# Relative positions in attention: 32 windows of the table against one row of queries each, or the whole tables against all queries and a diagonal read from DRAM

## The chip, the core and the metric

The kernel runs on one core of a Trainium2 chip. The metric is the device time of one execution in microseconds (us), taken over several runs. The engines are TensorE (PE, with its weight loads PEld), VectorE (DVE), ScalarE (ACT), GpSimd (POOL) and SyncE (SP, which issues most of the DMAs).

## The reference

The input `x` is 8 images of 32 x 32 positions with 384 channels. Layer 0 is a group norm, then self-attention over all 1024 positions of an image with 6 heads of 64, and a residual. The score has two relative terms, one for rows and one for columns:

```python
attn  = einsum('bqd,bkd->bqk', q * SCALE, k)
Rh    = rel_pos_h[i - j + 31]          # (32, 32, 64), a row per (query row i, key row j)
Rw    = rel_pos_w[i - j + 31]
rel_h = einsum('bhwc,hkc->bhwk', q, Rh)   # query (h, w) with key row k
rel_w = einsum('bhwc,wkc->bhwk', q, Rw)   # query (h, w) with key column k
attn[h, w, kh, kw] += rel_h[h, w, kh] + rel_w[h, w, kw]
out   = softmax(attn) @ v @ proj_w + proj_b
```

Layer 1 is a layer norm with causal attention over the 1024 tokens (one head of 384), and for the first five images an FFN of 384 x 1536 with binarized weights and a rescaling by the largest absolute value. The position tables have 63 rows of 64 each. A term depends on the query and on the difference of the two coordinates alone, so each query needs its product with 32 of the 63 rows.

## The kernel before, in words

The kernel works through the images one after the other in `run`. For each: `layer0` (projections, relative positions, attention), `attention1`, for images 0 to 4 `ffn`, and four DMAs on SP that store the result (L857). `between` normalises the next image in the middle of `attention1`. The order of instructions on each engine is fixed when the program is built, and it need not be that of the code: in the trace, some query projections of an image run while the FFN of the image before is still going on. Each engine then takes its own queue in order.

In `layer0`, `queries_keys(m)` projects 128 columns of queries (m = 0 to 2) or keys (m = 3 to 5), two heads at a time (a pair `p`; `par` is the head within the pair). L429 (ScalarE) rounds the product to float32r, and L430 (VectorE) stores what the rounding left. So `q[par]` has a rounded part in one half of its 128 partitions and the rest in the other half, and so have the keys. L442 and L443 (POOL) copy the keys with the halves exchanged (`ks`).

`positions(g)` takes four rows (d = 0) or columns (d = 1) of queries. For each of the four, for both heads and both tables, one plain fp32 matmul (L454) multiplies a window of 32 rows of the table with 96 queries (32 positions of the three pairs) and writes 32 partitions of PSUM. That is 16 matmuls per group and 128 per image. Then L464 (ScalarE) rounds the result to float32r and L465 (VectorE) stores the rest, both into `r[par]`, four times each per group, 32 times each per image. `values(j)` projects 128 positions of `v`, copied out of PSUM by L470, on ScalarE and VectorE in turn.

`attend0_fast` takes the pairs one after the other. For each 128 keys (a chunk `c`) and each head, L508 makes scores of 128 x 1024 in PSUM with three float32r matmuls per half: keys with queries, exchanged keys with queries, and `unit` with `r`. `unit` (made on POOL by `make_unit`) is a 0/1 matrix that gives each key its row's and its column's term. L512 takes the exponential on ScalarE, L521 sums on VectorE, and L526 multiplies with `v`. Two score tiles (`s_tile`, two banks of PSUM each) and four tiles of one bank (`o_tile`) exist; the position products use an `o_tile`. `page` is a pool of eleven SBUF tiles of 128 x 1024, used by the exponentials, the sums and, in the FFN, by the rounded activations. SP also loads the residual (L105), and the next image (L294). In the FFN's end, POOL clamps the output (L834), and VectorE adds it (L835), after which the stores L857 go out.

Of the kernel before, what the change touches and what calls it, by code (L numbers as in the profile page):

```python
# [17 lines left out]
P = 128  # L18
B, H, W, C = 8, 32, 32, 384
T = H * W  # L20
NJ = T // P
NC = C // P
NH, HD = 6, 64
NPAIR = NH // 2
# [50 lines left out]
def conv_attn_hybrid(  # L75
# [19 lines left out]
    nc = tc.nc  # L95
    assert GSB == 1
    const = ctx.enter_context(tc.tile_pool(name="const", bufs=1))
# [10 lines left out]
    def tile_of(name, shape):  # L108
        return const.tile(shape, F32, name=name)
# [1 line left out]
    wqkv_sb, wproj_sb, wv_sb = (tile_of(n, [P, NC, w]) for n, w in (("wqkv_sb", 3 * C), ("wproj_sb", C), ("wv_sb", C)))  # L111
    bqk, bv, b1_sb = (tile_of(n, [P, w]) for n, w in (("bqk", 6), ("bv", NC), ("b1_sb", NM)))
    pb, b2_sb = tile_of("pb", [P, C]), tile_of("b2_sb", [P, C])
    rel = tile_of("rel", [P, 2, 2 * H - 1])
    qscale = HD**-0.5

    def load_weights():

        nc.scalar.dma_start(out=bqk, in_=qkv_b[0 : 2 * C].rearrange("(m p) -> p m", p=P))
        for half in range(2):  # L120
            nc.scalar.dma_start(out=rel[half * HD : (half + 1) * HD, 0, :], in_=rel_hT)
            nc.scalar.dma_start(out=rel[half * HD : (half + 1) * HD, 1, :], in_=rel_wT)
        nc.scalar.dma_start(out=bv, in_=qkv_b[2 * C : 3 * C].rearrange("(m p) -> p m", p=P))
        nc.scalar.dma_start(out=b1_sb, in_=b1.rearrange("(m p) -> p m", p=P))
        src = qkv_w.rearrange("(k p) o -> p k o", p=P)
        for i in range(3):
            nc.sync.dma_start(out=wqkv_sb[:, :, ts(i, C)], in_=src[:, :, ts(i, C)])
        nc.sync.dma_start(out=wproj_sb, in_=proj_w.rearrange("(k p) o -> p k o", p=P))
        nc.sync.dma_start(out=pb, in_=proj_b.partition_broadcast(P))
        nc.sync.dma_start(out=wv_sb, in_=wv.rearrange("(k p) o -> p k o", p=P))  # L130
        nc.sync.dma_start(out=b2_sb, in_=b2.partition_broadcast(P))

        nc.scalar.mul(wqkv_sb[:, :, 0:C], wqkv_sb[:, :, 0:C], qscale)
        nc.scalar.mul(bqk[:, 0:NPAIR], bqk[:, 0:NPAIR], qscale)
        nc.scalar.mul(rel, rel, 1.0 / qscale)


    ident = const.tile([P, P], F32, name="ident")
# [8 lines left out]
    fold = const.tile([P, 2, 32], F32, name="fold")  # L147
    for i in range(2):
        nc.vector.tensor_reduce(fold[:, i, :], ident.rearrange("p (k i) -> p i k", k=4), AX.X, ALU.add)
    ones = const.tile([P, P], F32, name="ones")  # L150
    nc.gpsimd.memset(ones, 1.0)

    to_group = const.tile([P, NC, GROUPS_GN], F32, name="to_group")
# [21 lines left out]
    def make_unit():  # L175

        for i in range(4):
            r = slice(32 * i, 32 * (i + 1))
            nc.gpsimd.tensor_copy(
                unit[r].rearrange("i (h w) -> i h w", h=H), ident[r, r].unsqueeze(2 - i % 2).to_broadcast([32, H, W])  # L180
            )


# [3 lines left out]

    def judge(pools):

        bad = const.tile([P, 2, N_SEEN], F32, name="bad")  # L190
# [89 lines left out]
    def stages(pools):  # L280
# [140 lines left out]
        def layer0(b, xT):  # L421

            q, k, ks, r = ([pools.image(f"{n}_{b}_{par}", F32R) for par in range(2)] for n in ("q", "k", "ks", "r"))

            def hi_lo(dst, hi, lo, ps, bias):
                nc.scalar.activation(dst[hi], ps[hi], AF.Identity, bias=bias[hi])  # L429
                nc.vector.scalar_tensor_tensor(dst[lo], ps[hi], bias[hi], dst[hi].bitcast(F32), ALU.add, ALU.subtract)  # L430

            rows = (slice(0, HD), slice(HD, P))

            def queries_keys(m):
                p = m % NPAIR
                ps = project_T(wqkv_sb, ts(m, P), xT, f"qk_{b}_{m}")
                for par in range(2):
                    hi, lo = rows[par], rows[1 - par]
                    dst = (q if m < NPAIR else k)[par][:, p, :]
                    hi_lo(dst, hi, lo, ps, bqk[:, m : m + 1])  # L440
                    if m >= NPAIR:
                        nc.gpsimd.tensor_copy(ks[par][hi, p, :], dst[lo].bitcast(F32))  # L442
                        nc.gpsimd.tensor_copy(ks[par][lo, p, :], dst[hi].bitcast(F32))  # L443

            def positions(g):

                ps = pools.o_tile(f"rel_{b}_{g}")[:, :384].rearrange("p (i n) -> p i n", i=4)
                for i in range(4):
                    at = 4 * g + i
                    win = slice(H - 1 - at, 2 * H - 1 - at)  # L450
                    for par in range(2):
                        qv = q[par].bitcast(F32).rearrange("d p (h w) -> d p h w", h=H)
                        for d in range(2):
                            nc.tensor.matmul(  # L454
                                ps[ts(2 * par + d, 32), i, :], rel[:, d, win], qv[:, :, :, at] if d else qv[:, :, at, :],
                                start=True, stop=True,
                            )
                for d in range(2):
                    for par in range(2):
                        hi, lo = 2 * par + d, 2 * (1 - par) + d  # L460
                        dst = r[par].rearrange("k p (h w) -> k p h w", h=H)
                        dst = dst[:, :, :, ts(g, 4)] if d else dst[:, :, ts(g, 4), :]
                        src = ps[ts(hi, 32)].rearrange("k i (p t) -> k p t i" if d else "k i (p t) -> k p i t", p=NPAIR)
                        nc.scalar.copy(dst[ts(hi, 32)], src)  # L464
                        nc.vector.tensor_tensor(dst[ts(lo, 32)], src, dst[ts(hi, 32)].bitcast(F32), ALU.subtract)  # L465

            v = pools.flat(f"v0_{b}")[:, : NJ * C].rearrange("p (j c) -> p j c", j=NJ)

            def values(j):
                (nc.vector.tensor_copy if j % 2 else nc.scalar.copy)(  # L470
                    v[:, j, :], project(wqkv_sb, slice(2 * C, 3 * C), xT, j, f"v0_{b}_{j}")
                )

            for m in range(NPAIR):
                queries_keys(m)

            queries_keys(NPAIR)
            for g in range(NJ):
                positions(g)
                if g in (1, 3):  # L480
                    queries_keys(NPAIR + 1 + g // 2)
                values(g)
            if pools.fast and b == 0:
                join_biases(pools)
# [12 lines left out]
            return (attend0_fast if pools.fast else attend0_general)(residual, b, sides, v)  # L497

        def attend0_fast(residual, b, sides, v):
# [62 lines left out]
            def finish(p, sums, avs):  # L562

                tr = pools.page(f"tr0_{b}_{p}")
                for half in range(2):
                    den = pools.o_tile(f"den0_{b}_{p}_{half}")
                    for par in range(2):
                        nc.tensor.matmul(  # L568
                            den[ts(par, HD), :], ones[:, :HD], sums[par][:, ts(half, 512)], start=True, stop=True
                        )  # L570
# [266 lines left out]
        def run(pools):  # L837
            gn = load_T(0)
            if pools.fast:
                load_weights()  # L840
            gn = group_norm_T(0, gn)
            if pools.fast:
                make_unit()
# [62 lines left out]
```

## Time and profile before

| | |
|---|---|
| time, median of three runs | 2678.16 us (2672.93 to 2678.53) |
| the profiled execution | 2677.02 us, of which the span of the trace 2675.2 us |
| TensorE busy | 2574.3 us, 96% of the span |
| VectorE, ScalarE, POOL busy | 1496.3, 1056.5, 215.6 us |
| granted TensorE clock | 0.99 of full speed |
| DMA | 82.0 MB, 31 GB/s over the span |

A group row names a line, an engine, an operation, the tile written and the tiles read with partitions x elements, the count, then the total busy time in us and the mean in ns of one instruction, and after the second bar the time that the engine sat idle just before it and for what. A wait row names who waited for whom, the total in us, the number of times and the longest. Tiles of the main path have the prefix f_. Two records of one matmul line can belong to one call: the count in a row is of records.

### The profile page before, as it was taken

Reading aid. Unit: us, or ns where it says so; the run is one execution under the profiler, and the core shown is the slowest. Engines: PE = TensorE matmul, PEld = TensorE weight load, DVE = VectorE, ACT = ScalarE, POOL = GpSimd, SP = SyncE. Lnnn points to the kernel's source line nnn. Section 1 sums busy time; section 2 is a strip of 40 time slices with the busy share of each in tenths; the row PEclk is TensorE's granted clock in tenths of the full one; section 3 lists DMA queues with packets and bytes.
Section 4 is the critical chain, followed back from the end, with each engine's and each line's share of the span. In section 5 each row is a group of like instructions: output and inputs, shape, how many; then the busy total and the mean of one; then the engine's idle time right before and its main releaser. Section 6 shows DMA issues by size and latency. Waiting matters only on the chain.

```text
span 2675.2 us, 28350 instructions
## 1 busy us (share of the span) xinstructions
PE 2574.3 (96%) x11394; PEld 1546.7 (58%) x11394; DVE 1496.3 (56%) x2368; ACT 1056.5 (39%) x1470; POOL 215.6 (8%) x202
## 2 busy tenths in 40 slices
PE   8989999999999999999999999999999999999998
PEld 4554585555765556755558555576555555555554
DVE  4885456663565644666545666346664356425652
ACT  3431274431555414654127443155541254115411
POOL 2010004000030000120000400003000020002000
PEclk9999999999999999999999999999999999999999
DMA  2501101010010101010110101001000100010000
GB/s 93 201 35 59 36 1 48 1 60 33 4 48 1 48 12 36 12 36 1 59 36 1 48 1 59 3 33 48 1 24 0 48 1 0 24 48 1 1 1 25
DMA packets 34572, 82.00 MB, mean 31 GB/s; under 512 B 5120, under 2 KB 27520, under 8 KB 32896
## 3 DMA queue, kind: packets, MB, share of 16 engines
q1 hardware_dynamic: 28496, 56.43, 5.9%
q0 software_dynamic: 2880, 23.59, 2.6%
q8 instruction: 92, 1.51, 0.2%
q10 hardware_dynamic: 3056, 0.08, 0.1%
q14 instruction: 48, 0.39, 0.0%
HBM read 62.79 MB, written 17.30 MB: 30 GB/s over the span
## 4 chain that ended last, share of the span: by engine, by line
PE 88%; DVE 6%; ACT 2%; issue 1%; POOL 1%; DMA 1%; ACTq 0%; SPq 0%; DVEq 0%
PE f_s L508 19%; PE f_av L526 12%; PE f_v L385 8%; PE f_qk L375 8%; PE f_s L680 7%; PE f_av L694 7%; PE f_y L784 6%; PE f_y L821 6%; PE f_q L659 5%; PE f_pj L385 4%; PE f_rel L454 3%; POOL f_y L834 1%; PE f_pt L287 1%; DVE f_r L465 1%; PE f_den L568 1%
## 5 line engine op out<-in xcount | busy, mean ns | idle before, releaser
L512 ACT ACTIVATE f_pr<-f_s 128x1024 f32<-128x1024 f32 x384 | 393.6, 1026 | 446.0 <-PE f_s L508 429.9
L521 DVE TENSOR_TENSOR f_sum<-f_sum,f_pr 128x1024 f32<-128x1024 f32 x288 | 355.4, 1247 | 228.6 <-ACT f_pr L512 226.7
L526 PE MATMUL f_av<-f_pr,f_v 128*64 128x512 f32 x1536 | 351.8, 598 | 0.0
L508 PE MATMUL f_s<-f_q,f_k 128*128 128x512 f32 x768 | 258.0, 415 | 13.2 <-ACT f_pr L512 13.1
L375 PE MATMUL f_qk<-f_gnT,wqkv_sb 128*128 128x512 f32 x576 | 265.4, 607 | 1.2 <-DVE f_gnT L336 1.2
L508 PE MATMUL f_s<-f_r,unit 128*128 128x512 f32 x768 | 242.8, 397 | 2.5 <-DVE f_r L465 2.5
L508 PE MATMUL f_s<-f_q,f_ks 128*128 128x512 f32 x768 | 242.4, 397 | 0.0
L526 PEld LDWEIGHTS f_av<-f_pr,f_v 128*64 128x64 f32 x1536 | 101.9, 136 | 200.0 <-issue 192.2
L680 PE MATMUL f_s<-f_q,f_lnT 128*128 128x512 f32 (+3 forms) x576 | 200.1, 491 | 0.0
L694 PE MATMUL f_av<-f_v,f_pr 128*128 128x385 f32 x576 | 194.5, 486 | 0.0
L508 PEld LDWEIGHTS f_s<-f_q,f_k 128*128 128x128 f32 x768 | 125.4, 189 | 118.8 <-issue 48.7
L375 PEld LDWEIGHTS f_qk<-f_gnT,wqkv_sb 128*128 128x128 f32 x576 | 108.3, 194 | 123.6 <-issue 121.3
L465 DVE TENSOR_TENSOR f_r<-f_rel,f_r 32x384 fp32r<-32x384 f32 x256 | 139.7, 553 | 52.7 <-ACT f_r L464 46.7
L508 PEld LDWEIGHTS f_s<-f_r,unit 128*128 128x128 f32 x768 | 144.0, 189 | 40.4 <-DVE f_r L465 6.8
L508 PEld LDWEIGHTS f_s<-f_q,f_ks 128*128 128x128 f32 x768 | 145.2, 189 | 35.0
L694 PEld LDWEIGHTS f_av<-f_v,f_pr 128*128 128x128 f32 x576 | 108.6, 190 | 78.6 <-issue 11.5
L680 PEld LDWEIGHTS f_s<-f_q,f_lnT 128*128 128x128 f32 x576 | 100.7, 190 | 71.5 <-issue 47.4
L464 ACT CAST f_r<-f_rel 32x384 fp32r<-32x384 f32 x256 | 118.8, 469 | 50.8 <-PE f_rel L454 26.3
L385 PE MATMUL f_v<-wqkv_sb,f_gnT 128*128 128x384 f32 x384 | 137.9, 495 | 0.0
L385 PE MATMUL f_pj<-wproj_sb,f_oT 128*128 128x384 f32 x384 | 128.1, 490 | 9.6 <-DVE f_oT L574 9.6
L788 ACT ACTIVATE f_h<-f_y,b_sb 128x256 f32<-128x256 f32 x240 | 101.7, 472 | 69.0 <-PE f_y L784 38.0
L659 PE MATMUL f_q<-f_lnT,wqk 128*128 128x512 f32 x288 | 127.9, 598 | 0.0
(156 smaller groups left out, 3371.2 us busy)
## 6 DMA issues: line engine op xcount, KB each, us to landing
f_gnT<-in_xT SPq DMA_DIRECT2D x24, 512.0 KB, 4.6
f_x<-in_x SPq DMA_DIRECT2D x32, 384.0 KB, 4.5
out_y<-f_x SPq DMA_DIRECT2D x32, 384.0 KB, 2.5
f_w1a<-w1s POOLq DMA_DIRECT2D x5, 1536.0 KB, 7.2
f_w2a<-w2s POOLq DMA_DIRECT2D x5, 1536.0 KB, 6.8
f_wrest<-w1s POOLq DMA_DIRECT2D x5, 768.0 KB, 4.6
f_wrest<-w2s POOLq DMA_DIRECT2D x5, 768.0 KB, 8.4
wqkv_sb<-in_qkv_w SPq DMA_DIRECT2D x3, 576.0 KB, 5.8
```

Of the source, the lines that this page charges most:

```text
L375: nc.tensor.matmul(ps[:, half, :], w[:, k, cols], xT[:, k, ts(half, 512)], start=(k == 0), stop=(k == NC - 1),)
L385: nc.tensor.matmul(ps[:, :C], xT[:, k, ts(j, P)], w[:, k, cols], start=(k == 0), stop=(k == NC - 1))
L465: nc.vector.tensor_tensor(dst[ts(lo, 32)], src, dst[ts(hi, 32)].bitcast(F32), ALU.subtract)
L508: nc.tensor.matmul(sc[:, half, :], keys[:, ts(c, P)], queries[:, ts(half, 512)], start=(i == 0), stop=(i == 2))
L512: nc.scalar.activation(pr, sc.rearrange("p a n -> p (a n)"), AF.Exp)
L521: nc.vector.tensor_tensor(sums[par], prev, prs[par], ALU.add)
L526: nc.tensor.matmul(avs[half][ts(par, HD), :], v[:, c, ts(h, HD)], prs[par][:, ts(half, 512)], start=(c == 0), stop=(c == NJ - 1),)
L659: nc.tensor.matmul(ps, wqk[:, k, ts(m, P)], xT[:, half, k, :], start=(k == 0), stop=(k == NC - 1))
L680: nc.tensor.matmul(sc[:, half, lo:], xT[:, c // 4, k, ts(c % 4, P)], q[:, half, k, lo:], start=(k == 0), stop=(k == NC - 1),)
L694: nc.tensor.matmul(av[:, : C + 1], prs[c][:, ts(j - c, P)], v[:, c, :], start=(c == 0), stop=(c == j))
L784: nc.tensor.matmul(ps, w1k[i // 2][:, ts(m, P)], xs[i % 2][:, half, i // 2, :], start=(i == 0), stop=(i == 2 * NC - 1))
L821: nc.tensor.matmul(ps[:, :C], hs[i][:, m, :], w2m[half * 6 + m], start=(half == m == i == 0), stop=(half == i == 1 and m == 5),)
```

## The change

The position products are no longer made window by window. `rel_split` holds both tables, 63 rows and one of zeros each, side by side as 128 columns, once rounded to float32r and once what the rounding left. `positions(p)` now works on a pair: for each head and each half of the positions, two float32r matmuls (one with each part of `rel_split`, summed in PSUM) multiply all 128 table rows with 512 queries. ScalarE copies the 64 rows of the first table to a page, and VectorE the 64 rows of the second, with the positions transposed so that columns come first. The page is stored to DRAM (`far`) by one DMA of 512 KB on SP. Then, for each head and table, one DMA on SP reads from `far` the diagonal of 32 x 32 pieces of 32 numbers that the 32 windows stand for, into a quarter of another page, `near`. A new function, `split`, rounds this to float32r on ScalarE and stores the rest on VectorE into `r`, once per pair, head and table, 1024 numbers per partition each. The diagonal gives the keys' coordinate in the opposite order, so `unit` is built reversed, and the tables are no longer reversed on the host.

In the order of the code, `positions(p)` stands after `queries_keys(p + 1)`, all key projections come before all of `values`, and the splits stand before `values(0)`, after `values(3)` and after `values(7)`. `ones` is cut to 64 columns, `bad` becomes a page, and `rel` a page of the start.

```diff
-    rel = tile_of("rel", [P, 2, 2 * H - 1])
+    rel_split = const.tile([P, 2, 2, 2 * H], F32R, name="rel_split")
...
+        rel = pools.page("rel")[:, : 4 * H].rearrange("p (d i) -> p d i", d=2)
+        nc.vector.memset(rel, 0.0)
...
         nc.scalar.mul(rel, rel, 1.0 / qscale)
+        nc.scalar.copy(rel_split[:, 0], rel)
+        nc.vector.tensor_tensor(rel_split[:, 1], rel, rel_split[:, 0].bitcast(F32), ALU.subtract)
...
-                unit[r].rearrange("i (h w) -> i h w", h=H), ident[r, r].unsqueeze(2 - i % 2).to_broadcast([32, H, W])
+                unit[r].rearrange("i (h w) -> i h w", h=H),
+                ident[r, r][:, ::-1].unsqueeze(2 - i % 2).to_broadcast([32, H, W]),
...
-            def positions(g):
-                ps = pools.o_tile(f"rel_{b}_{g}")[:, :384].rearrange("p (i n) -> p i n", i=4)
-                for i in range(4):
-                    at = 4 * g + i
-                    win = slice(H - 1 - at, 2 * H - 1 - at)
-                    for par in range(2):
-                        qv = q[par].bitcast(F32).rearrange("d p (h w) -> d p h w", h=H)
-                        for d in range(2):
+            def positions(p):
+                fars = []
+                for par in range(2):
+                    page = pools.page(f"far_{b}_{p}_{par}")
+                    by_col = page.rearrange("i (w h) -> i w h", h=H)
+                    for half in range(2):
+                        ps = pools.o_tile(f"rel_{b}_{p}_{par}_{half}")
+                        for i in range(2):
                             nc.tensor.matmul(
-                                ps[ts(2 * par + d, 32), i, :], rel[:, d, win], qv[:, :, :, at] if d else qv[:, :, at, :],
-                                start=True, stop=True,
+                                ps, rel_split[:, i].rearrange("d a n -> d (a n)"), q[par][:, p, ts(half, 512)],
+                                start=(i == 0), stop=(i == 1),
                             )
+                        nc.scalar.copy(page[:HD, ts(half, 512)], ps[:HD])
+                        nc.vector.tensor_copy(
+                            by_col[HD:, :, ts(half, H // 2)], ps[HD:].rearrange("i (h w) -> i w h", w=W)
+                        )
+                    far = store.tile([P, T], F32, tag=f"far_{p}_{par}", bufs=2, name=f"{pools.path}_far_{b}_{p}_{par}")
+                    nc.sync.dma_start(out=far, in_=page)
+                    fars.append(far)
+                near = pools.page(f"near_{b}_{p}")
+                for par in range(2):
+                    start = fars[par][0:1, 0:1]
+                    for d in range(2):
+                        src = bass.AP(start.tensor, start.offset + d * HD * T, [[T, 32], [T + 32, 32], [1, 32]])
+                        nc.sync.dma_start(
+                            out=near[ts(2 * par + d, 32)].rearrange("m (n o) -> m n o", n=32), in_=src
+                        )
+                return near
+
+            def split(p, near):
                 for d in range(2):
                     for par in range(2):
                         hi, lo = 2 * par + d, 2 * (1 - par) + d
-                        dst = r[par].rearrange("k p (h w) -> k p h w", h=H)
-                        dst = dst[:, :, :, ts(g, 4)] if d else dst[:, :, ts(g, 4), :]
-                        src = ps[ts(hi, 32)].rearrange("k i (p t) -> k p t i" if d else "k i (p t) -> k p i t", p=NPAIR)
+                        dst = r[par][:, p, :].rearrange("k (h w) -> k h w", h=H)
+                        src = near[ts(hi, 32)].rearrange("k (w h) -> k h w" if d else "k (h w) -> k h w", h=H)
                         nc.scalar.copy(dst[ts(hi, 32)], src)
                         nc.vector.tensor_tensor(dst[ts(lo, 32)], src, dst[ts(hi, 32)].bitcast(F32), ALU.subtract)
...
-            for m in range(NPAIR):
+            near = []
+            for m in range(2 * NPAIR):
                 queries_keys(m)
-
-            queries_keys(NPAIR)
-            for g in range(NJ):
-                positions(g)
-                if g in (1, 3):
-                    queries_keys(NPAIR + 1 + g // 2)
-                values(g)
+                if 0 < m <= NPAIR:
+                    near.append(positions(m - 1))
+            split(0, near[0])
+            for j in range(NJ):
+                values(j)
+                if j % 4 == 3:
+                    split(1 + j // 4, near[1 + j // 4])
```

More of the change, by code (lines that the diff above doesn't have):

```diff
@@ L113, in conv_attn_hybrid, with load_weights @@
     pb, b2_sb = tile_of("pb", [P, C]), tile_of("b2_sb", [P, C])
-    rel = tile_of("rel", [P, 2, 2 * H - 1])
+    rel_split = const.tile([P, 2, 2, 2 * H], F32R, name="rel_split")
     qscale = HD**-0.5
-    def load_weights():
+    def load_weights(pools):
         nc.scalar.dma_start(out=bqk, in_=qkv_b[0 : 2 * C].rearrange("(m p) -> p m", p=P))
+        rel = pools.page("rel")[:, : 4 * H].rearrange("p (d i) -> p d i", d=2)
+        nc.vector.memset(rel, 0.0)
         for half in range(2):
-            nc.scalar.dma_start(out=rel[half * HD : (half + 1) * HD, 0, :], in_=rel_hT)
-            nc.scalar.dma_start(out=rel[half * HD : (half + 1) * HD, 1, :], in_=rel_wT)
+            nc.scalar.dma_start(out=rel[half * HD : (half + 1) * HD, 0, : 2 * H - 1], in_=rel_hT)
+            nc.scalar.dma_start(out=rel[half * HD : (half + 1) * HD, 1, : 2 * W - 1], in_=rel_wT)
         nc.scalar.dma_start(out=bv, in_=qkv_b[2 * C : 3 * C].rearrange("(m p) -> p m", p=P))
@@ L149, in conv_attn_hybrid @@
         nc.vector.tensor_reduce(fold[:, i, :], ident.rearrange("p (k i) -> p i k", k=4), AX.X, ALU.add)
-    ones = const.tile([P, P], F32, name="ones")
+    ones = const.tile([P, HD], F32, name="ones")
     nc.gpsimd.memset(ones, 1.0)
@@ L188, in judge @@
     def judge(pools):
-        bad = const.tile([P, 2, N_SEEN], F32, name="bad")
+        bad = pools.page("bad")[:, : 2 * N_SEEN].rearrange("p (i n) -> p i n", i=2)
         for i, most in enumerate((SUM_MAX, RSUM_MAX)):
@@ L568, in finish @@
                         nc.tensor.matmul(
-                            den[ts(par, HD), :], ones[:, :HD], sums[par][:, ts(half, 512)], start=True, stop=True
+                            den[ts(par, HD), :], ones, sums[par][:, ts(half, 512)], start=True, stop=True
                         )
@@ L839, in run @@
             if pools.fast:
-                load_weights()
+                load_weights(pools)
             gn = group_norm_T(0, gn)
@@ L884 @@
         "proj_b": L0_conv_proj_b,
-        "rel_hT": np.asarray(L0_conv_rel_pos_h)[::-1].T,
-        "rel_wT": np.asarray(L0_conv_rel_pos_w)[::-1].T,
+        "rel_hT": np.asarray(L0_conv_rel_pos_h).T,
+        "rel_wT": np.asarray(L0_conv_rel_pos_w).T,
         "wqT": np.asarray(L1_attn_Wq).T,
```

## The prediction

> **What bounds the kernel now.** First the page's busy row and the chain of waits:
>
> ```profile
> PE 2574.3 (96%) x11394; PEld 1546.7 (58%) x11394; DVE 1496.3 (56%) x2368; ACT 1056.5 (39%) x1470; POOL 215.6 (8%) x202
> ...
> PE 88%; DVE 6%; ACT 2%; issue 1%; POOL 1%; DMA 1%; ACTq 0%; SPq 0%; DVEq 0%
> PE f_s L508 19%; PE f_av L526 12%; PE f_v L385 8%; PE f_qk L375 8%; PE f_s L680 7%; PE f_av L694 7%; PE f_y L784 6%; PE f_y L821 6%; PE f_q L659 5%; PE f_pj L385 4%; PE f_rel L454 3%; POOL f_y L834 1%; PE f_pt L287 1%; DVE f_r L465 1%; PE f_den L568 1%
> ```
>
> TensorE sets the end: 88% of the chain is its work, 3% (80 us) of it the position matmuls (L454) that the change replaces. Next, whether this holds in the stage concerned. The windows view (columns: stretch, length, busy us of each engine, clock, DMA) of the projections and the attention of image 2 (it follows an FFN) and image 6 (it doesn't):
>
> ```profile
> 763.00:814.00 51.00, 48.18 (x351) 25.81 (x349) 35.60 (x57) 24.58 (x42) 27.14 (x22) 0.97 0.18 63
> 814.00:924.00 110.00, 108.62 (x471) 62.99 (x470) 66.78 (x64) 52.21 (x54) 0.11 (x1) 1.00 0.00 1
> 2108.00:2168.00 60.00, 60.00 (x378) 30.73 (x377) 33.96 (x49) 29.29 (x46) 19.12 (x13) 1.00 0.10 34
> ```
>
> Image 6: TensorE has no gap in 60 us; VectorE (third figure) has 34, ScalarE 29. Image 2: the stage is shorter because some query projections ran inside the FFN, and TensorE lacks 2.8 us. The waits view says why:
>
> ```profile
> PE f_rel L454 <- ACT f_v L470: 15.1, 5, 3.4
> ...
> SPq L857 <- DVE f_x L835: 1064.8, 20, 208.0
> ```
>
> That is one wait of about 3 us after each of the five FFNs: in the timeline POOL's clamp (L834) runs from 772.0 to 779.7, VectorE's L835 waits on it until 781.2, and the casts behind it, then TensorE, wait too. SP's output stores (L857) wait for the same L835, to 781.6. The attention windows have room: VectorE 67 of 110 us.
>
> **What the Trainium skill says.** (1) "DMA: Bandwidth & Descriptors", Two DMAs through the same engine are not ordered: a DMA that reads what another wrote must wait for its semaphore. So SP must stand still between storing `far` and reading it. (2) Same page, Specifications: transfers under 512 B miss line rate. The new pieces have 128 B. The trace's DMA view of 0 to 12 us agrees only partly that small packets are bad: 15.4% of 16 engines x 12 us over 3056 packets is 9.7 ns each. (3) "TensorEngine Tiling (Array Packing)", Key Properties: changing the tiling mode drains the array; the old 32-column matmuls switch twice per group. No row shows that by itself; the spacing below contains it. (4) "VectorE: DVE Perf Modes", Why `tensor_tensor` can't do 2x_2P or 4x: an fp32 subtraction goes at one element per cycle. L521 agrees: 1247 ns for 1024.
>
> **TensorE, removed and added.** The timeline of image 6:
>
> ```profile
> 2129.26 1.52 PE L454 MATMUL f_rel<-f_q,rel 128*32 128x96 f32 x32
> 2130.71 2.20 PE L385 MATMUL f_v<-wqkv_sb,f_gnT 128*128 128x384 f32 x6
> ```
>
> A group of 16 old matmuls holds TensorE for 1.45 us (start to next start); eight groups are 11.6 us per image. A plain fp32 matmul leaves two records (32 for 16 calls). The new ones have float32r on both sides, like L508, whose 512-column matmuls leave one record each:
>
> ```profile
> 2172.35 0.63 PE L508 MATMUL f_s<-f_q,f_ks 128*128 128x512 f32 x2
> 2172.82 0.63 PE L508 MATMUL f_s<-f_r,unit 128*128 128x512 f32 x2
> ```
>
> Two every 0.47 us, 0.235 each. New: 3 pairs x 2 heads x 2 halves x 2 table parts = 24 matmuls, 24 x 0.235 = 5.6 us. Each needs its own weights, 0.19 us on PEld, inside 0.235. Saved: 6.0 us per image, 47.7 us in all.
>
> **ScalarE and VectorE.** The rows used (last numbers: total, mean ns | idle before):
>
> ```profile
> L465 DVE TENSOR_TENSOR f_r<-f_rel,f_r 32x384 fp32r<-32x384 f32 x256 | 139.7, 553 | 52.7 <-ACT f_r L464 46.7
> L464 ACT CAST f_r<-f_rel 32x384 fp32r<-32x384 f32 x256 | 118.8, 469 | 50.8 <-PE f_rel L454 26.3 <-DVE f_r L465 13.4
> L545 ACT COPY f_oT<-f_av 128x512 f32<-128x512 f32 x32 | 18.7, 587 | 29.8 <-PE f_av L526 29.8
> L660 DVE COPY f_q<-f_q 128x512 f32<-128x512 f32 x32 | 22.1, 692 | 102.3 <-PE f_q L659 102.3
> ```
>
> ScalarE loses 32 x 0.469 = 15.0 us per image and gets 12 copies (as L545) 7.0 plus 12 splitting copies of 1024 from SBUF, about 1.06 each (L133: 1152 in 1163 ns), 12.7: up 4.7. VectorE loses 32 x 0.553 = 17.7 and gets 12 copies (as L660) 8.3 plus 12 subtractions (as L521) 15.0: up 5.6. In image 6 that is 34 and 40 us beside 54 of TensorE: no cost, TensorE's work hides it. The strided addresses (32-element steps) have no row of their own; L465 reads with such steps and shows no penalty, so I take none, at most twice the 6 split copies of one table on each engine, still hidden there. The table split at the start and the reversed `unit` (POOL) lie beside the first loads: 0 to 0.5 us.
>
> After an FFN it is tighter. VectorE is blocked to 781.2, and then has keys 7.7 (6 x 1.28), copies still open 5.6 (two pairs), splits 15.0, `v` copies 2.2: 30.5 us, to 812. TensorE, with 48.2 - 12.2 (L454's busy time there) + 5.6 = 41.6 us of work left at 763 and its 2.8 us wait, is done by 807. The last split pair (5 us) isn't needed until the third head pair, some 70 us later, and VectorE gains in the attention (67 of 110), so I charge 1 us per FFN image, with 0 to 6 as bounds.
>
> **DMAs.** Per image SP gets 6 stores of 512 KB and 12 reads. A 384 KB store lands in 2.5 us (L857), so about 3. Each read issues in about 0.5 us (L105: four in 1.92). A pair's four reads are 4 x 1024 packets of 128 B, 256 per engine. Bounds for a packet: 9.7 ns as above (mean 26 B), 88.6 ns from queue q1 (5.9% of 16 x 2675 us over 28496 packets of 1980 B). So a pair's reads take R = 2.5 to 22.7 us; I take 14 ns, 3.6 us, because q1's time per byte (0.045 ns) adds only 4.6 ns to the small packet's 9.7. Queued behind SP's waits are only the residual load (L105; needed 40 us later) and output stores. In image 6 the first positions are ready 12 us into the stage, the third near 27, with their copies at 31; store 3, reads 4 plus 2 to land: at 40, and scores start at 54. All hidden. After an FFN, stores may queue behind L857 until 781.6, and the third pair arrives at about 785 + 3 x 3.6 + 2 = 798: before 807.
>
> **Sum.** Images 0, 6, 7: 3 x 6.0 = 18, plus 0.3 each for the first score's wait for `f_r` (2.5 us over seven), whose split now comes early: 19. Images 1 to 5: 5 x (6.0 - 1) = 25. Back 4 for the VectorE backlog at eight attention starts. Net 40. The profiled execution took 2677.0 us (span 2675.2), 1.1 under the median of 2678.2: 2677.0 - 40 + 1.1 = 2638.
>
> **Rivals.**
> - *The pieces come late (slower).* One mechanism: ScalarE's queue is in order, the third pair's split (4.2 us) may stand ahead of the first exponential, and TensorE has two score tiles (2.8 us) before it stops. After an FFN scores start at 808 (807 and the 1 us charged), so it needs 785 + 3R + 2 <= 808 + 2.8 - 4.2, R <= 6.5 us; in image 6, with the first store landed at 19, 19 + 3R + 2 <= 54 + 2.8 - 4.2, R <= 10.5. Beyond that each us of R costs 3 per image. It eats the 40 us at 15(R - 6.5) = 40, R = 9.2 us, or 36 ns per packet; at R = 12 it is 5 x 16.5 + 3 x 4.5 - 40 = 56 slower: 2734. For: 128 B pieces, SP standing behind L857. Against: 9.7 ns. Chance 0.15.
> - *VectorE becomes the bound after an FFN.* At its bound of 6 us images 1 to 5 gain nothing: 2678 - 19 + 4 = 2663; with PSUM tiles held by blocked copies at a further 3 us each, no change. For: 30.5 us of queue from 781. Against: 10 of it can be late. Chance 0.16, of it 0.04 within 0.2%.
> - *The new matmuls don't run as float32r* but leave two records each, at L375's 0.43: 24 x 0.86 = 20.6, 9 us more per image, 2750. Against: L508's rows. Chance 0.02, with the splits' strides at twice their price 0.02 more.
> - *Better than that:* the 3 us wait goes too, 2677 - 48 - 15 = 2614. Chance 0.03.
>
> **How the numbers follow.** Forecast: 0.62, 2625 to 2655. With VectorE's case (0.12 of it still faster) and the better one: faster 0.77, same 0.04, slower 0.19. A measurement of this kernel tells about 0.2% (5 us) from no change. Range: 2616 to 2690, taking in the partial case and the mild end of late pieces.
>
> **What would show it.** Right: the position matmuls at 192 records, one per call, spaced 0.235; image 6's stage at 54 us without gaps; `near` landing within 6 us; no exponential waiting on it. Wrong: first scores (L508) waiting on an exponential (L512) that stands behind a split of `near`; packets over 36 ns; TensorE's wait after an FFN above 5 us.

## The result and the profile after

The changed kernel took 2686.72 us (median of four runs, 2683.09 to 2687.28) against 2678.35 for the kernel before beside it: a ratio of 1.0033, with a 95% interval of 1.0016 to 1.0051. It is slower by 8 us where 40 us less were forecast. Its profiled execution has a span of 2681.3 us. First the busy row of the page, and three rows of the groups view (total, mean ns | idle before):

```profile
PE 2546.6 (95%) x9538; PEld 1528.4 (57%) x9538; DVE 1610.9 (60%) x2306; ACT 1128.9 (42%) x1407; POOL 253.5 (9%) x202
...
L492 DVE TENSOR_TENSOR f_r<-f_near,f_r 32x1024 fp32r<-32x1024 f32 x96 | 197.4, 2057 | 31.5 <-ACT f_r L491 29.0
L491 ACT CAST f_r<-f_near 32x1024 fp32r<-32x1024 f32 x96 | 147.0, 1532 | 2.3
L464 PE MATMUL f_rel<-f_q,rel_split 128*128 128x512 f32 x192 | 65.5, 476 | 35.8 <-DVE f_q L436 35.8
```

TensorE's position work is there as planned: 192 records. But its last figure is new: 35.8 us of idling ahead of these matmuls, for VectorE's conversion of the queries (L436). The waits view of the whole run gives the second place as well (in all, times, longest):

```profile
PE f_v L391 <- DVE f_far L469: 17.8, 7, 3.6
```

The lengths of the images, from the end of one `pj` (the output projection of `layer0`) to the next, worked out from the traces, in us. Images 1 to 5 have an FFN ahead of them, 0, 6 and 7 don't:

| image | 0 | 1 | 2 | 3 | 4 | 5 | 6 | 7 |
|---|---|---|---|---|---|---|---|---|
| before | 231.9 | 356.9 | 358.5 | 358.0 | 358.8 | 358.5 | 278.3 | 279.3 |
| after | 222.5 | 363.8 | 365.1 | 365.1 | 361.7 | 362.1 | 274.3 | 272.6 |

So the images without an FFN gained 9.4 + 4.0 + 6.7 = 20.1 us, and the others lost 27.1. The windows view of image 6 after, from its first key or query projection to its first score, and of image 2 from the end of its predecessor's FFN for 56 us and the 110 us behind them, show the same:

```profile
2127.60:2180.20 52.60, 52.37 (x147) 27.35 (x146) 39.23 (x40) 33.00 (x36) 18.66 (x13) 1.00 0.49 128
762.00:818.00 56.00, 45.40 (x121) 24.40 (x120) 42.00 (x47) 29.59 (x33) 29.10 (x22) 0.88 0.53 141
818.00:928.00 110.00, 109.48 (x465) 62.61 (x464) 75.48 (x66) 56.29 (x56) 2.66 (x2) 1.00 0.00 1
```

Image 6 is full (52.4 of 52.6 us). Image 2 lacks over 10 us of TensorE, and the clock is 0.88. VectorE's timeline of image 2, and POOL's, show what TensorE waits for:

```profile
764.04 0.35 POOL L775 PARTITION_ALL_REDUCE qa<-qg  x1 [44.80 <-DVE qg L773]
771.35 7.70 POOL L862 TENSOR_SCALAR f_y<-f_y,qu,ql 128x384 f32<-128x384 f32 x8 [6.96 <-issue]
```

```profile
768.31 1.28 DVE L436 SCALAR_TENSOR_TENSOR f_q<-f_qk,bqk,f_q 64x1024 fp32r<-64x1024 f32 x1 [1.51 <-ACT f_q L435]
769.61 1.91 DVE L469 COPY f_far<-f_rel 64x512 f32<-64x512 f32 x3
772.03 1.56 DVE L863 SCALAR_TENSOR_TENSOR f_x<-f_y,qs,f_x 128x384 f32<-128x384 f32 x2 [0.50 <-POOL f_y L862]
...
779.08 1.48 DVE L863 SCALAR_TENSOR_TENSOR f_x<-f_y,qs,f_x 128x384 f32<-128x384 f32 x1 [0.40 <-POOL f_y L862]
780.59 1.29 DVE L436 SCALAR_TENSOR_TENSOR f_q<-f_qk,bqk,f_q 64x1024 fp32r<-64x1024 f32 x1
...
798.14 1.28 DVE L436 SCALAR_TENSOR_TENSOR f_k<-f_qk,bqk,f_k 64x1024 fp32r<-64x1024 f32 x1
799.45 2.52 DVE L469 COPY f_far<-f_rel 64x512 f32<-64x512 f32 x4
```

The third pair of queries has two conversions. The first stands at 768.3, the second at 780.6, with the eight adds L863 between them, which wait piece by piece for POOL's clamp L862. In the kernel before, both conversions stood ahead of the eight adds (there L835), in its image 2:

```profile
767.62 1.28 DVE L430 SCALAR_TENSOR_TENSOR f_q<-f_qk,bqk,f_q 64x1024 fp32r<-64x1024 f32 x1 [2.15 <-ACT f_q L429]
770.08 1.29 DVE L430 SCALAR_TENSOR_TENSOR f_q<-f_qk,bqk,f_q 64x1024 fp32r<-64x1024 f32 x1 [1.18 <-ACT f_q L429]
772.71 1.56 DVE L835 SCALAR_TENSOR_TENSOR f_x<-f_y,qs,f_x 128x384 f32<-128x384 f32 x2 [1.34 <-POOL f_y L834]
```

The order is made when the program is built. The copies L469, which this change brings to VectorE, stand among these instructions too, but that they pushed the second conversion back is not shown: in a run below it stands behind the adds with no copy of a product on VectorE. The position matmuls of the third pair need the second conversion, so TensorE waits 7.0 us. The second place is the last of VectorE's rows above: the copies of the third pair's products stand at 799.4, behind five of the keys' conversions and four splits (L492) of the first pair, hold their PSUM tiles until then, and TensorE's `v` waits 3.6 us for one of these.

**Where the time went.** The gaps of over 0.15 us between TensorE's records were added up. The loss by the clock is (1 - granted clock) x time. Over the whole span it is 26 us before and 52 us after, but 5 and 17 us of it fall into the gaps, where a low clock costs nothing, so it is counted only where TensorE works. What is left is TensorE's work at full clock:

| us | span | gaps | clock | rest |
|---|---|---|---|---|
| before | 2675.2 | 100.8 | 21.8 | 2552.6 |
| after | 2681.3 | 134.3 | 34.7 | 2512.3 |

The work is 40 us less, and gaps (+33.5) and clock (+12.9) give 46 back.

### The profile page after: what moved, and what is told of

The parts are those of the page before. It is cut to its first block, busy times and chain, and to the rows that moved or that the text cites. A ratio compares the mean times of both kernels' runs of the same rounds, so it can differ in the third digit from the quotient of the medians.

```text
span 2681.3 us, 24809 instructions
## 1 busy us (share of the span) xinstructions
PE 2546.6 (95%) x9538; PEld 1528.4 (57%) x9538; DVE 1610.9 (60%) x2306; ACT 1128.9 (42%) x1407; POOL 253.5 (9%) x202
## 5 line engine op out<-in xcount | busy, mean ns | idle before, releaser
L549 DVE TENSOR_TENSOR f_sum<-f_sum,f_pr 128x1024 f32<-128x1024 f32 x288 | 346.1, 1222 | 180.8 <-ACT f_pr L540 178.2
L554 PE MATMUL f_av<-f_pr,f_v 128*64 128x512 f32 x1536 | 367.0, 599 | 0.0
L536 PE MATMUL f_s<-f_q,f_k 128*128 128x512 f32 x768 | 256.4, 415 | 11.8 <-ACT f_pr L540 11.6
L492 DVE TENSOR_TENSOR f_r<-f_near,f_r 32x1024 fp32r<-32x1024 f32 x96 | 197.4, 2057 | 31.5 <-ACT f_r L491 29.0
L491 ACT CAST f_r<-f_near 32x1024 fp32r<-32x1024 f32 x96 | 147.0, 1532 | 2.3
L823 DVE TENSOR_REDUCE am<-f_h 128x1 f32<-128x1024 f32 (+2 forms) x80 | 72.5, 948 | 97.2 <-ACT f_h L816 97.2
```

The costliest lines, as they stand in the source:

```text
L536: nc.tensor.matmul(sc[:, half, :], keys[:, ts(c, P)], queries[:, ts(half, 512)], start=(i == 0), stop=(i == 2))
L549: nc.vector.tensor_tensor(sums[par], prev, prs[par], ALU.add)
L554: nc.tensor.matmul(avs[half][ts(par, HD), :], v[:, c, ts(h, HD)], prs[par][:, ts(half, 512)], start=(c == 0), stop=(c == NJ - 1),)
L823: nc.vector.tensor_reduce(am[:, i, n - 1 : n], pairs[i][:, :, cuts[n - 1] : cuts[n], :], AX.XYZ, ALU.max, apply_absolute_value=True)
```

## The experiments

Three theories were stated first. **Blocked queue:** VectorE's order after an FFN, with conversions and copies that TensorE needs behind instructions that wait, takes the time. **Late pieces:** the way of the products through DRAM takes it. **Overload:** ScalarE and VectorE have too much to do, at first because of the strided splits; in the later runs this became the sum of VectorE's work. Times are medians beside 2677 to 2680 us for the kernel before on the same chip.

**Clamp on VectorE.** The adds then wait for nobody.

```
-    nc.gpsimd.tensor_scalar(y[:, j, :], y[:, j, :], up, low, ALU.min, ALU.max)
+    nc.vector.tensor_scalar(y[:, j, :], y[:, j, :], up, low, ALU.min, ALU.max)
```

> The kernel after the change, with the clamp of the FFN's output (L862) on VectorE instead of POOL. Theory (blocked queue): after each FFN VectorE's eight adds L863 wait for POOL's clamp, which starts 7 us after the maximum is known, and the conversion of the third pair's queries stands behind them, so TensorE idles 7 us, then works at half clock and idles 3.6 us more. With the clamp on VectorE nothing waits for POOL: the 7 us wait falls to about 3, and the kernel gets 20 to 40 us faster than after the change (2687), to 2647 to 2667. Rival (late pieces: the round trip through DRAM sets the time): no change, 2682 to 2692. Rival (ScalarE and VectorE overloaded by splits that read with a stride): VectorE gets 8 x 0.4 us per FFN more to do, so no gain or up to 15 us slower.

Measured: 2654.76 us, ratio 0.9914 (0.9899 to 0.9929). TensorE's waits in the same 70 us after the FFN:

```profile
PE f_s L536 <- DVE f_k L436: 2.6, 1, 2.6
PE f_rel L464 <- DVE f_far L469: 2.2, 1, 2.2
PE f_rel L464 <- DVE f_q L436: 1.3, 1, 1.3
```

The wait of 7.0 us is down to 2.2 + 1.3, and in place of the 3.6 us for `v` there are 2.6 for the keys. The images behind an FFN last 357.8 to 358.8 us, those without one are unchanged. In this build the adds stand ahead of both conversions, so the place behind them is not by itself the cause: it is that they waited for POOL. They now end 11.3 us after the FFN's last reduction, and 17.5 us after it in the changed kernel. That is worth 32 us of 2687, though VectorE's busy time over the run is as good as unchanged (1607.5 us, 1610.9 in the changed kernel).

**The same edit in the kernel before**, a control.

> Control: the kernel before the change, with its clamp L834 on VectorE. Blocked queue: the 3 us waits of TensorE after each of the five FFNs go, 10 to 15 us faster than 2678, so 2663 to 2668; that is less than the change of e1 brings, because the kernel before had only keys behind the adds. The other theories say nothing of this kernel; if it gains as much as e1, the clamp's cost has nothing to do with the change.

Measured: 2681.65 us, 1.0018 (1.0011 to 1.0025). A miss: no gain. In this build the clamps and adds stand ahead of both conversions of the third pair, and TensorE waits for them as long as before:

```profile
PE f_rel L454 <- DVE f_q L430: 2.7, 1, 2.7
```

So the edit itself is no gain. Here it takes POOL's clamp out of VectorE's queue, but it also puts the clamps and adds ahead of conversions that had stood in front of them.

**Products two groups later.**

```
-    if 0 < m <= NPAIR:
-        near.append(positions(m - 1))
+    if m >= NPAIR:
+        near.append(positions(m - NPAIR))
```

> The kernel after the change, with positions(p) called after queries_keys(p + 3) instead of p + 1, so that all three query conversions stand ahead of the blocked adds, as they did before the change. Clamp stays on POOL. Blocked queue: the 7 us wait and the half clock after it go in five images, 25 to 45 us faster than after (2687): 2642 to 2662. Late pieces: the products are made and stored 10 us later, so this is slower than after, by up to 5 x 10 us: 2690 to 2737. Overload by strided splits: the same work, no change, 2680 to 2692.

Measured: 2715.73 us, 1.0146 (1.0127 to 1.0164). The blocked queue's forecast failed, that of late pieces holds. The built order did put both conversions ahead of the adds, but the copies came behind them instead (4.6 us), and scores wait for keys and for `r`:

```profile
PE f_rel L464 <- DVE f_far L469: 4.6, 1, 4.6
PE f_s L536 <- DVE f_r L492: 4.0, 2, 2.1
PE f_s L536 <- DVE f_k L436: 2.3, 1, 2.3
```

The images without an FFN lost 12.3, 6.4 and 7.5 us against the changed kernel.

**Products one group later** (`if 2 <= m < 2 + NPAIR: near.append(positions(m - 2))`).

> The changed kernel with the products of a pair of heads made one group of queries or keys later (if 2 <= m < 2 + NPAIR: positions(m - 2)): the queue of VectorE then holds both conversions of the third pair of queries ahead of the eight adds that wait for the clamp. Blocked queue: TensorE's wait of 7 us for that conversion behind each FFN shrinks to 3 us or less, the half clock after it with it; five images gain 4 to 7 us each and image 0, 6 and 7 nothing: 2650 to 2667 us. Late pieces (two later cost the images without an FFN ahead of them 6.4 to 12.5 us each): one later costs about half of that, 3 to 6 us in each of the eight images, and the wait after an FFN moves on rather than goes: 2690 to 2705 us.

Measured: 2699.46 us, 1.0081 (1.0067 to 1.0094). Inside what late pieces said, but not for its reason: images 0, 6 and 7 lost 9.1, 7.5 and 7.2 us, nearly what two groups cost, and not half. Image 7's waits in the 50 us of its last projections show one of 5.5 us, and it is for VectorE's queue, not for a transfer:

```profile
PE f_s L536 <- DVE f_k L436: 5.5, 1, 5.5
```

In this build TensorE has the first scores ahead of most of `v` (in image 7 they begin 122.4 us into the image, 137.9 in the changed kernel), and the last keys' conversions stand between splits. Moving a step in the code moved other things in the built order. Neither of these two runs isolates the place of the conversion, which they were made for.

**Without the way through DRAM.** The stores and reads of `far` and `near` are removed, and the split reads the page of the products directly, so the diagonal is left out.

> The kernel after the change without the 6 stores and 12 reads per image: split takes the page of one head as it stands (the diagonal is left out, so the positions are not those of the reference). In the built order the third pair's query conversion still stands behind the adds. Late pieces: all of the loss goes, 40 us or more faster than after, about 2645. Blocked queue: the 7 us wait stays, within 10 us of after: 2677 to 2692. Overload by strided splits: unchanged, within 5 us.

Measured: 2648.62 us, 0.9899 (0.9884 to 0.9915), as late pieces said. The trace contradicts it, though: the transfers that were removed had been fast and nobody had waited long for them (the DMA issues and two rows of waits of the changed kernel; L491, which reads `near`, idled 2.3 us in all):

```profile
f_far<-f_far SPq DMA_DIRECT2D x48, 512.0 KB, 3.3
f_near<-f_far SPq DMA_DIRECT2D x96, 128.0 KB, 3.8
...
SPq L480 <- DMA f_far<-f_far: 33.8, 40, 2.7
```

And the kernel without them keeps the first wait and has lost the second (L526 and L530 are its scores and exponentials):

```profile
PE f_rel L464 <- DVE f_q L436: 7.1, 1, 7.1
PE f_s L526 <- ACT f_pr L530: 1.5, 1, 1.5
```

Its built order has all copies ahead of the splits. These waits are not the whole of its gain: an image behind an FFN is 6.6 us shorter than in the changed kernel, and 2.7 us of that are gaps (table at the end of this section). The next runs test whether that order is enough with the transfers in place.

**Contiguous reads in the split**, with the step of 128 bytes on the side that writes.

```
-    dst = r[par][:, p, :].rearrange("k (h w) -> k h w", h=H)
-    src = near[ts(hi, 32)].rearrange("k (w h) -> k h w" if d else "k (h w) -> k h w", h=H)
+    dst = r[par][:, p, :].rearrange("k (h w) -> k w h" if d else "k (h w) -> k h w", h=H)
+    src = near[ts(hi, 32)].rearrange("k (a c) -> k a c", a=H)
```

> The changed kernel with one edit in split: near is read in its own order, and the copy to r and the subtraction write with the 128-byte step instead. Strided reads as the price: in the changed kernel the strided subtractions on VectorE take 1.95 us and more against 1.21 us for the contiguous ones, and ScalarE's copies 2.0 against 1.04 us. If reading is what costs, the subtractions fall to about 1.2 us, VectorE gets 6 x 0.75 = 4.5 us per image back, of which an image behind an FFN, where VectorE is behind, shows 2 to 4 us: 2665 to 2677 us. The blocked queue (q's second conversion behind the eight adds): that order stays, the wait of 7 us stays, 2680 to 2690 us. If a strided write costs what a strided read does, the subtractions stay near 2 us and the time does not move.

Measured: 2684.62 us, 1.003 (1.0019 to 1.0041): no change. The row of the subtractions says why:

```profile
L492 DVE TENSOR_TENSOR f_r<-f_near,f_r 32x1024 fp32r<-32x1024 f32 x96 | 201.7, 2101 | 28.3 <-ACT f_r L491 25.9
```

A strided write costs what a strided read does. What the strides cost in time of the kernel this run couldn't tell.

**Splits later**, so that the third pair's copies come ahead of the first split.

```
-    split(0, near[0])
     for j in range(NJ):
         values(j)
-        if j % 4 == 3:
-            split(1 + j // 4, near[1 + j // 4])
+        if j in (3, 5, 7):
+            split(j // 2 - 1, near[j // 2 - 1])
```

> The changed kernel with the splits of the three pairs after the fourth, sixth and eighth group of v (before: after the last keys, and after the fourth and the eighth group of v): in VectorE's queue pair 2's copies of the products then stand ahead of pair 0's subtractions. Blocked queue, second place: TensorE's second wait behind an FFN, 2.9 to 3.6 us for a v tile behind those copies, goes, and the kernel without the trip through DRAM (2648.6 us) won by its order; the first wait of 7 us stays: 2665 to 2676 us. Late pieces: r is made later than before, the first scores of an image wait for it by up to 4 x 1.3 to 2 us in eight images: 2700 to 2735 us. No effect of the order: within 4 us of 2686.

Measured: 2675.47 us, 0.9986 (0.9979 to 0.9993), at the upper end of the blocked queue's range. The second wait falls from 3.6 to 2.1 us and a wait of 1.3 for an exponential appears; the first stays at 7.0. Order alone is worth 11 us here, a third of what removing the transfers gave.

**VectorE's half of the copies on ScalarE**, clamp left on POOL.

```
-    nc.vector.tensor_copy(
+    nc.scalar.copy(
         by_col[HD:, :, ts(half, H // 2)], ps[HD:].rearrange("i (h w) -> i w h", w=W)
     )
```

> The changed kernel with VectorE's half of the copies of the products on ScalarE, and the clamp left on POOL. In VectorE's queue the eight adds still stand between the two conversions of the third pair of queries, but no copy of a product stands anywhere on VectorE. Blocked queue: the wait of 7 us for the second conversion stays in five images, the second wait of 2.9 to 3.6 us, for a v tile behind pair 2's copies, goes: 5 x 3.6 = 18 us and some half clock, 2660 to 2672 us. VectorE's sum of work (12 x 0.69 = 8.3 us per image less) as the cause: the images behind an FFN gain about 8 us as in the kernel with the clamp moved too, 2640 to 2652 us. Nothing from either: 2680 or more.

Measured: 2650.61 us, 0.9886 (0.9869 to 0.9904). That is inside the range of VectorE's sum of work and below that of the blocked queue. The waits, though, are those that the blocked queue forecast:

```profile
PE f_rel L464 <- DVE f_q L436: 6.5, 1, 6.5
PE f_v L391 <- ACT f_far L469: 1.1, 1, 1.1
```

The first wait is as good as whole, the second is nearly gone, and the time is that of the kernel without the transfers (2648.62), with all transfers in place. That takes the ground from late pieces. The gain of 36 us is about twice what the waits alone say: of 6.4 us per image behind an FFN 3.5 are gaps, 1.6 the clock, and 1.3 closer matmuls. So this run doesn't decide between the order and the sum of VectorE's work. It does show that the second conversion of the third pair's queries stays behind the eight adds (at 773.9, the adds from 765.4 on) when VectorE has no copy of a product.

**Both: clamp on VectorE and the copies on ScalarE.**

> The changed kernel with the clamp on VectorE (2654.8 us by itself) and with VectorE's half of the copies of the products on ScalarE as well. VectorE behind after an FFN: its 12 copies of 0.69 us are 8.3 us per image less for it while it is late by 1.3 to 2.6 us at three places; those waits go where ScalarE, busy 42% of the span, keeps up: 2640 to 2649 us. ScalarE becomes late instead (24 copies of 0.58 to 0.69 us in a row with its own conversions): the waits move to it, 2653 to 2670 us. If the time comes from the half clock and not from the waits, it follows them in either case.

Measured: **2634.76 us, 0.9839 (0.9825 to 0.9852)**, below the first range and the fastest of all. Windows of the 70 us behind the FFN (length, then busy us of TensorE, its loads, VectorE, ScalarE, POOL; then the clock), first the changed kernel, then this one:

```profile
762.00:832.00 70.00, 59.40 (x176) 32.49 (x175) 52.67 (x53) 40.11 (x43) 31.65 (x22) 0.90 0.42 113
```

```profile
754.30:824.30 70.00, 65.94 (x211) 36.02 (x210) 55.98 (x55) 53.99 (x59) 23.35 (x14) 0.98 0.42 113
```

TensorE has 6.5 us more of work in it, at 0.98 of the clock instead of 0.90. VectorE is no less busy in these 70 us than in the changed kernel; over the whole run it has less to do (1555.1 us busy against 1610.9). The images behind an FFN last 352.9 to 354.7 us, on average 4.0 us less than in the kernel before and 9.4 less than in the changed one. One wait is left:

```profile
PE f_s L536 <- DVE f_k L436: 3.8, 1, 3.8
PE f_rel L464 <- ACT f_far L469: 0.2, 1, 0.2
```

**Both, and the splits later**, to take away that wait.

> The changed kernel with three edits together: the clamp on VectorE, VectorE's half of the copies of the products on ScalarE, and the splits after the fourth, sixth and eighth group of v. With the first two alone the time was 2634.8 us, and one wait of 3.8 us was left in an image behind an FFN: TensorE at the scores for the last keys' conversion, which stood behind splits in VectorE's queue. Here the eight conversions stand ahead of all splits. Blocked queue: that wait goes in five images, with some 1 us each for the half clock after it: 2608 to 2618 us. Late pieces: r is made later and the first scores wait for it instead, 1 to 3 us in each of eight images: 2630 to 2655 us.

Measured: 2663.84 us, 0.9935 (0.9921 to 0.995). A miss, 29 us slower than without the third edit. The wait for keys is gone, and another stands in its place (L535 and L539 are its scores and exponentials):

```profile
PE f_s L535 <- ACT f_pr L539: 4.3, 2, 3.8
```

With `r` late, the built order completes the first score tile behind all of `v` instead of ahead of it, and the first exponential stands behind later splits in ScalarE's queue. It begins at 808.5, 4.6 us after the end of `v`; without the third edit it began as `v` ended (802.4 and 802.5). TensorE, with both score tiles full, stops for it. What late pieces said happened, by a place in the order again.

**Control: the kernel before with the clamp on VectorE and its `v` copies on ScalarE.**

> A control. The kernel before with the clamp on VectorE and its four copies of v per image on ScalarE: VectorE is relieved there too, though its copies of products do not exist in this kernel (the splits read PSUM). What the two moves give the changed kernel (52 us) could be owed to them alone and not to the change. If so the kernel before gains as well: 2640 to 2660 us. If the change's own saving on TensorE was only covered up by VectorE's queue, the kernel before has nothing covered up and stays within 8 us of its 2678 us: its wait after an FFN is 2.7 us, and the clamp alone left it at 2681.7.

Measured: 2680.34 us, 1.0004 (0.9994 to 1.0015). The two moves give the kernel before nothing in this form. So the 43.5 us by which the best version beats it (2678.25 to 2634.76) are not owed to moves that any version would gain from. TensorE's wait of 2.7 us after an FFN stayed in both controls, so a form of the kernel before that is rid of it was not tried.

**The images behind an FFN side by side**, counted as in the table further up: means of images 1 to 5 in the profiled executions. That of the changed kernel took 3.6 us less than its median, that of the later splits 7 us less.

| us per image | length | gaps | clock | rest |
|---|---|---|---|---|
| kernel before | 358.1 | 11.8 | 2.8 | 343.5 |
| changed kernel | 363.6 | 18.5 | 6.0 | 339.1 |
| clamp on VectorE | 358.4 | 13.3 | 6.1 | 339.0 |
| without the way through DRAM | 356.9 | 15.8 | 4.3 | 336.8 |
| splits later | 360.8 | 17.7 | 5.1 | 338.0 |
| copies on ScalarE | 357.2 | 15.0 | 4.4 | 337.8 |
| both | 354.1 | 11.1 | 4.7 | 338.3 |
| both, and splits later | 358.3 | 12.9 | 5.4 | 339.9 |

The clamp's gain lies in the gaps alone. In the best version the gaps are back at those of the kernel before, and TensorE's saving shows in the time. The rest differs by up to 3 us between versions with the same matmuls; why is open.

## Why the prediction was wrong

- **TensorE's work: right in kind, somewhat too large.** The rest of the table above fell by 40 us, where 48 were forecast: by 6.1 us per image without an FFN (forecast 6.0), by 4.4 behind one. The spacing was off: the eight position matmuls of a pair took 2.26 us from their start to the next projection in image 6, 0.28 each and not 0.235. Images 0, 6 and 7 gained 20.1 us in length where the sum has 19, but that close match is in part luck: image 0 alone gained 9.4, of which 2.6 are a higher clock, and images 6 and 7 gained 10.7 together where the sum has over 12.
- **The transfers: right.** A read of `near` landed 3.8 us after its issue (5.5 at most), within the 6 us that were named, and its packets of 128 bytes took 13 ns in the median, where 14 were taken. The rival of late pieces falls with that, and with the kernel that keeps the transfers and runs at 2650.61.
- **"No penalty" for strided addresses: wrong.** Subtractions are 1.21 us contiguous and 1.95 strided, and in seven of the eight images one takes 6.6 to 7.9; ScalarE's copies are 1.04 and 2.0. Per image VectorE's twelve took 24.7 us, not 15.0 (the strides alone make 19; the rest is mostly that long one), and ScalarE's 18.4, not 12.7. In images without an FFN TensorE's work hid it. Behind an FFN it lies ahead of the third pair's copies, but how much of the loss is due to it wasn't measured.
- **The step that failed:** "TensorE, with ... its 2.8 us wait, is done by 807", and with it "I charge 1 us per FFN image, with 0 to 6 as bounds". The forecast was -5 us for each of these images and the trace shows +5.4 (27.1 / 5), so the sum was 10.4 us too low, five times: 52 us. In its place the runs showed 6.7 us more of gaps (two waits of 7.0 and 3.6 us where there had been 2.8 and 1.0), 3.1 us more lost by the clock, and 4.4 us less work instead of 6.0. The working added up VectorE's work from 781.2 on (keys, copies, splits, `v`) and held it against a deadline. The second conversion of the third pair's queries is not in that list: before, it stood ahead of the adds that wait for POOL, and the working took it for granted that it stays there. Nor did it ask where the new copies would stand, and they came behind four splits. Why the built order put the conversion behind the adds stays open.
- **Its own sign of being wrong** came: "TensorE's wait after an FFN above 5 us". The nearest rival was VectorE after an FFN with PSUM tiles held by blocked copies "at a further 3 us each": that is the second wait. It ended at no change because the longer first wait and the clock were not in it. A slower kernel had 0.19, most of it for late pieces, so what was forecast for that side rested on a mechanism that did not occur.
- **Shown and not shown.** That the loss sits in VectorE's queue behind the FFN is shown by the runs that take most of either wait away (-32 and -36 us) or both (-52), and by the controls. That POOL's clamp standing in that queue is the larger part is shown by the clamp on VectorE: the same busy time of VectorE, and 5.2 us less gaps per image. For the second wait, order and sum of work are separated only in part: the later splits change the order alone and gain 11 us, but the moved copies, which gain 36, change both. The trial of moving the conversion alone, with all else in its place, did not succeed: both attempts also changed other places of the built order.

## What to carry to other kernels

When a change brings new instructions to an engine whose queue stands still for another engine, ask which of the neighbours' instructions they will push behind the stall, and who waits for those: a sum of work against a deadline doesn't tell. A gain on the bounding engine can be real and still be given back at one join; compare the stages with and without that join before the change is dropped. Here two edits to what stands in VectorE's queue, which gave the old kernel nothing in the form that fits it, turned a loss of 8 us into a gain of 43.

## What the hardware showed that was not expected

- A step of 128 bytes in SBUF makes an fp32 instruction of 32 x 1024 take nearly twice as long on ScalarE (1.04 to 2.0 us) and 1.6 times on VectorE (1.21 to 1.95), on the reading side as on the writing one. The Trainium skill has it: "SBUF — State Buffer", in the box on cachelines of the section Door 1, names 16-byte lines and so four fp32 elements as the step that is free. This case agrees, with 32 elements at 1.6 to 1.9 times the time. The prediction took the old kernel's steps in PSUM (L465) as its evidence, and those did not carry over to SBUF: the new copies L469 read PSUM with the same step at no cost (0.69 us, as L660 without one).
- VectorE and POOL get in each other's way when both work from SBUF. In image 2 of the changed kernel the subtraction that begins during POOL's residual add took 7.09 us instead of 1.2 to 2. The numbers look as if it had stood still until POOL was done: POOL's add ends at 813.82 + 6.73 = 820.55, and the subtraction at 822.39, about one strided subtraction later.

```profile
813.82 6.73 POOL L519 TENSOR_TENSOR f_x<-f_x,pb 128x3072 f32<-128x3072 f32 x1 [8.38 <-DMA f_x<-in_x]
```

```profile
815.30 7.09 DVE L492 TENSOR_TENSOR f_r<-f_near,f_r 32x1024 fp32r<-32x1024 f32 x1
```

  POOL's casts L448 of 64 x 1024 took 1.04 us, and 2.08 where they began together with such a subtraction (at 786.4 and 792.3 in that image).
- POOL's clamp began 7 us after the reduction over partitions, though the last of its bounds (L860) was ready at 766.8, 4.6 us ahead of it (the 6.96 us of "issue" in POOL's row above).
- The clock was lower in stretches with TensorE's waits: 0.90 over the 70 us behind an FFN with waits of 7.0 and 3.6 us, 0.95 with 6.5 and 1.1, 0.98 with 3.8 alone. The Trainium skill, "TensorE: Matmul & The Clock Gate", Part 1, says that after an idle window of about 3.4 us the array runs at half rate until a busy one has passed. This case agrees in that image 2 of the changed kernel has a clock of 0.50 from 778.2 to 784.9 and from 798.7 to 805.4 us and of 1.00 between. Shorter waits do it too: a single one of 2.8 us in the kernel before was followed by 0.50 from 786.1 to 789.4, and waits of 2.2 and 1.3 us close together (the clamp on VectorE) by 0.50 from 772.0 to 778.7. The price is smaller than the mean clock says, because a part of the low stretch lies in the wait itself: 70 us at 0.90 are about 7 us lost, of which 4.1 fall where TensorE works.
